# Layer 0, images 1 to 7: scores as three one-pass products of 12-bit halves, two units in a batch, one bank of sums

## The chip, the cores and the metric

The kernel runs on one core of a Trainium2 chip. The metric is the device time of one execution in microseconds. Engines are named as in the profile: PE (TensorE: matmuls; PEld its weight loads), DVE (VectorE), ACT (ScalarE), POOL (GpSimd) and SP, whose queue issues nearly all DMAs. All work in parallel and meet at semaphores.

## The reference

Two layers act on 8 images of 384 channels and 32 x 32 = 1024 positions. Only the attention of layer 0 is touched:

```python
qkv = (tokens @ qkv_w + qkv_b).reshape(b, n, 3, NUM_HEADS, HEAD_DIM)   # n 1024, 8 heads of 48
q, k, v = (qkv[0], qkv[1], qkv[2])
attn = jnp.einsum('bhnd,bhmd->bhnm', q * scale, k)
attn = attn + _relative_bias(h, w, mlp_w1, mlp_b1, mlp_w2, mlp_b2)[None]
attn = jax.nn.softmax(attn, axis=-1)
out = jnp.einsum('bhnm,bhmd->bhnd', attn, v)
```

`tokens` is the image after a group norm. An output projection with a residual follows, then layer 1 (attention and a binarized feed-forward net), which this change leaves alone.

## The kernel before

**Units.** Heads go in four pairs, one head on partitions 0 to 63 and one on 64 to 127. Pairs 0 to 2 hold six heads; pair 3 (`NF0`) holds the last two, whose channels are computed as 16 spare rows beside each of the other heads (rows 48 to 63 of a half) and moved into place by DMA (`FR` = 16 rows at a time). A unit is a pair, a half of the 512 queries (`h`) and 256 of the keys (`m2`), two key tiles of 128. An image has 4 x 2 x 4 = 32 units.

**Scores and sums.** `scores` (L748) lays four tiles of 48 x 64 into PE's array at a time: two heads on its row halves, two runs of 64 keys on its column halves, in float32. DVE adds the position bias (L759, 128 x 1024, one instruction a head), ACT takes the exponential (L763). `weigh` multiplies the exponentials with v (L779), again in four tiles of 64 x 64: the two halves of the keys are summed in two PSUM banks, of which ACT copies one (L787) and DVE adds the other (L790). Row 0 of each head's result is the softmax's denominator, since v has columns of ones. `weigh` runs `LAG` = 2 units behind `scores`, so that PE always has sums to do while scores pass through DVE and ACT. PSUM has four buffers of two banks for everything: one holds the sums, three go round.

**Division.** When a pair is done, `divide` stores the denominators (L805), reads them back over 128 partitions (L807), inverts them on POOL (L808), stores and spreads them (L812, L820) and multiplies (L824). For pair 3 six DMAs (L834) then move rows into the spare rows of the others, for the output projection. These steps are spaced by `later`, a list of work due after so many calls of `later.step()`, one call a unit or a projection step.

**The next image's projections.** `Ahead` splits the normalized image into a high part (a mask on the bits, `mask`), a low part and a mixed part, each kept in a format that PE multiplies in one pass (`F32R`), and multiplies it with weights split in the same manner (`products`, L170). `BLOCKS` lists six blocks: three pairs, each for q and k. A block's products of mixed parts are in `pm`, those of high and low parts in `pg`; `take` joins them: ACT writes -`pm`/4096 + bias (L671), DVE adds `pg` (L675), two DMAs of 64 KB move the spare rows to pair 3 (L680). After three blocks `project_v` computes v (L700; DVE L708, L712), then the other three blocks follow. The image's scores start right after. The tiles of q and k lie in the pool `a_qk`: four buffers of 2 x 1024 numbers a partition, one for each pair. They also hold the image's high parts before.

**Order.** Every engine runs its instructions in the order in which the program issues them; the pools' buffers and the semaphores come from the framework. A buffer is given to a new tile when all that use the old one are done. Beside the units run, at fixed numbers: the loading of the next image (L343, `i` = 1), its group norm, the output projection of the image before (L847, at `i` = 3, 15.6 us of PE), the cutting of layer 1's weights (images 1 to 3) and the masks and roundings of the next image (`i` = 25 to 30). Image 0 has its own simpler projection (`project_qk`).

Of the kernel before, what the change touches and what calls it, by code (L numbers as in the profile page):

```python
# [22 lines left out]
ALU = mybir.AluOpType  # L23
# [251 lines left out]
def _layer0(tc, ins, x1, sums, shared, weights, beside):  # L275
# [9 lines left out]
    with ExitStack() as ctx:  # L285
        const = ctx.enter_context(tc.tile_pool(name="a_const", bufs=1))
        qkp = ctx.enter_context(tc.tile_pool(name="a_qk", bufs=NP0))
# [273 lines left out]
        def project_qk(b, xn):  # L561

            qk = {
                pair: qkp.tile([P, 2, N], F32, tag="qk", name=f"qk{b}_{pair}") for pair in range(NP0)
            }
            for pair in range(NF0):
                t = qk[pair]
                for s in range(2):
                    pq = mm2(f"pq{b}_{pair}_{s}")
# [11 lines left out]
                    if s == 0:  # L581
                        nc.vector.tensor_scalar(
                            t[:, s], flat2(pq), bias, D0**-0.5, ALU.add, ALU.mult
                        )
                    else:
                        nc.scalar.activation(t[:, s], flat2(pq), AF.Identity, bias=bias)
                    later.step()
                for j in range(2):
                    nc.sync.dma_start(
                        qk[NF0][j * S0 + pair * FR : j * S0 + (pair + 1) * FR],  # L590
                        t[j * S0 + D0 : (j + 1) * S0],
                    )
# [31 lines left out]
        class Ahead:  # L624
# [4 lines left out]
            def __init__(self, b, xn):  # L629
                self.b, self.xn = b, xn  # L630
                self.qk = {}
                self.parts, self.ps = [[], [], []], {}

            def tile(self, pair):
                if pair not in self.qk:
                    self.qk[pair] = qkp.tile([P, 2, N], F32, tag="qk", name=f"qk{self.b}_{pair}")
                return self.qk[pair]

            def high(self, k):
                return self.tile(k // 2)[:, k % 2]  # L640

            def mask(self, k):
                _masked(nc, self.high(k), self.xn[:, k])

            def round(self, k):
                t = etile(f"xh{self.b}_{k}", dtype=F32R)
                nc.scalar.copy(t, self.high(k))
                self.parts[0].append(t)

            def low(self, k):  # L650
                t = etile(f"xl{self.b}_{k}", dtype=F32R)
                nc.vector.tensor_sub(t, self.xn[:, k], self.high(k))
                self.parts[1].append(t)

            def mixed(self, k):
                t = etile(f"xd{self.b}_{k}", dtype=F32R)
                _mixed(nc, t, self.parts[1][k].bitcast(F32), self.high(k))
# [8 lines left out]
            def take(self, n):  # L666
                pair, s = BLOCKS[n]
                t = self.tile(pair)[:, s]
# [9 lines left out]
                last = self.tile(NF0)  # L678
                for j in range(2):
                    nc.sync.dma_start(  # L680
                        last[j * S0 + pair * FR : j * S0 + (pair + 1) * FR, s],
                        t[j * S0 + D0 : (j + 1) * S0],
                    )
                later.step()
# [56 lines left out]
        def scores(b, qk, u, weigh):  # L741
            pair, h, m2 = u
            s = [mm2(f"s{b}_{pair}_{h}_{m2}_{j}") for j in range(2)]
            for i in range(2):
                for c in range(2):
                    for j in range(2):
                        rows = slice(j * S0, j * S0 + D0)
                        nc.tensor.matmul(  # L748
                            s[j][ts(c, QP), i], qk[pair][rows, 1, ts(4 * m2 + 2 * i + c, QP)],
                            qk[pair][rows, 0, ts(h, HALF)], start=True, stop=True,  # L750
# [18 lines left out]
        def weigh(b, u, es):  # L769
# [24 lines left out]
            return finish  # L794

# [131 lines left out]
        for k, at in enumerate(((17, 22, 23), (21, 25, 26), (27, 30, 31))):  # L927
            for when, stage in zip(at, cut_weights_v(k)):
                later.after(when + 1, stage)
        for b in range(B):  # L930
            held = []
            for i, u in enumerate(units):
                done = held.pop(0) if len(held) == LAG else None
                held.append(
                    (u, scores(b, qk, u, lambda: weigh(b, *done) if done else None))
                )
                if i == (16 if b == 0 else 1) and b + 1 < B:
                    xn = load(b + 1)
                    for at, stage in zip(
                        (2, 3, 4, 6, 9, 10, 11) if b == 0 else (5, 6, 7, 10, 13, 13, 13),  # L940
# [35 lines left out]
            def weigh_held():  # L976
                finish = weigh(b, *held.pop(0))
                if finish is not None:
                    finish()
# [14 lines left out]
            weigh_held()  # L994
# [25 lines left out]
            qk = ahead.qk  # L1020
# [1352 lines left out]
```

## Time and profile before

| | us |
|---|---|
| median of 3 runs | 2943.4 (2942.52 to 2945.47) |
| profiled execution, its time | 2940.6 |
| its span in the trace | 2939.1 |
| PE busy | 2913.6 |
| DVE, ACT, POOL busy | 1969.8, 1504.5, 493.5 |
| one image of layer 0 (period of the stages) | 166.0 |
| of it: 32 units, output projection, next image's projections | 112.8, 15.6, 37.5 |
| score products (L748), sums (L779), all 8 images | 606.4, 603.5 |

The span is the time from the first to the last instruction in the trace; the 1.5 us to the execution's own time lie around it. Busy times of PE are those of matmuls that are pipelined, so a busy PE may still not be at its peak. In all 1060 DMAs move 209 MB.

### The profile page before, as it was taken

The numbers are of one execution on the slowest core, as the hardware profiler recorded it, in microseconds if no ns is written. First come the engines' busy times: TensorE is split into PE (matmuls) and PEld (weight loads), VectorE is DVE, ScalarE is ACT, GpSimd is POOL, SyncE is SP. The second block draws the span as 40 slices with busy tenths as digits, with TensorE's granted clock in tenths as the row PEclk, the third lists the DMA queues.
The fourth block names the chain that finished last, engine by engine and source line by source line (L and its number), as shares of the span: only waits on it lengthen the run. The fifth ranks groups of instructions, "written<-read, shape, count | busy, mean of one in ns | idle before, by whom it ended". The sixth has DMA issues, their size and how long they took to land.

```text
span 2939.1 us, 47521 instructions
## 1 busy us (share of the span) xinstructions
PE 2913.6 (99%) x19538; PEld 1703.0 (58%) x19538; DVE 1969.8 (67%) x1999; ACT 1504.5 (51%) x1846; POOL 493.5 (17%) x318
## 2 busy tenths in 40 slices
PE   8999999999999999999999999999999999999998
PEld 3465665657575666634546647647647647655553
DVE  3976758586676757573655775875875875875756
ACT  2644636264444636363643655555555555564644
POOL 3121202021110202012202202302302302311020
PEclk9999999999999999999999999999999999999999
DMA  7642131413122130323311212112112112112111
GB/s 191 197 147 84 50 111 46 121 45 98 47 74 73 39 113 24 100 69 107 78 56 31 84 31 72 67 32 72 67 32 72 67 32 72 67 40 83 40 46 39
DMA packets 131970, 214.35 MB, mean 73 GB/s; under 512 B 62144, under 2 KB 81072, under 8 KB 130368
## 3 DMA queue, kind: packets, MB, share of 16 engines
q1 hardware_dynamic: 128480, 209.39, 24.3%
q8 instruction: 157, 2.57, 0.4%
q10 hardware_dynamic: 3264, 1.82, 0.2%
q14 instruction: 69, 0.57, 0.1%
HBM read 161.83 MB, written 40.28 MB: 69 GB/s over the span
## 4 chain that ended last, share of the span: by engine, by line
PE 92%; DVE 3%; DMA 2%; ACT 2%; issue 1%; SPq 0%; POOL 0%; DVEq 0%; ACTq 0%
PE s L748 15%; PE o L779 15%; PE s L1725 11%; PE o L1774 10%; PE pg L170 6%; PE y2p L2019 6%; PE y1p L1968 5%; PE pp L847 4%; PE pv L1662 4%; PE pm L170 3%; PE pp L1871 3%; PE vg L700 2%; PE pq L1514 2%; PE pq L572 1%; DMA rb<-rd 1%
## 5 line engine op out<-in xcount | busy, mean ns | idle before, releaser
L763 ACT ACTIVATE e<-e 128x1024 f32<-128x1024 f32 x512 | 534.5, 1057 | 333.2 <-DVE e L759 316.7
L759 DVE TENSOR_TENSOR e<-s,grow 128x1024 f32<-128x1024 f32 x512 | 601.1, 1218 | 154.6 <-PE s L748 137.8
L748 PE MATMUL s<-qk 48*64 48x512 f32 x4096 | 606.4, 590 | 1.8 <-DVE e L759 1.8
L779 PE MATMUL o<-e,v 64*64 64x512 f32 x4096 | 603.5, 589 | 0.0
L1736 ACT ACTIVATE e<-s,kc 128x512 f32<-128x512 f32 x768 | 463.3, 693 | 173.5 <-PE s L1725 163.9
L1725 PE MATMUL s<-qk,qk 64*64 64x512 f32 x3072 | 419.4, 592 | 1.6 <-DVE oT L1784 1.3
L1774 PE MATMUL o<-e,v 64*64 64x512 f32 x3072 | 415.0, 590 | 0.0
L748 PEld LDWEIGHTS s<-qk 48*64 48x64 f32 x4096 | 231.7, 132 | 235.3 <-issue 98.7
L779 PEld LDWEIGHTS o<-e,v 64*64 64x64 f32 x4096 | 251.6, 133 | 188.4 <-issue 97.3
L1725 PEld LDWEIGHTS s<-qk,qk 64*64 64x64 f32 x3072 | 154.3, 132 | 191.5 <-issue 109.0
L1751 DVE TENSOR_TENSOR t<-t,e 128x1024 f32<-128x1024 f32 x192 | 230.9, 1221 | 45.6 <-ACT e L1736 45.4
L1774 PEld LDWEIGHTS o<-e,v 64*64 64x64 f32 x3072 | 160.5, 133 | 168.2 <-issue 141.9
L808 POOL TENSOR_TENSOR inv<-sums,over 128x16 f32<-128x16 f32 x32 | 95.8, 2992 | 843.9 <-DMA sums<-sd 776.8
L1955 DVE TENSOR_REDUCE parts<-y 128x1 f32<-128x1024 f32 x75 | 89.7, 1217 | 102.6 <-ACT y L1952 102.1
L1748 DVE TENSOR_TENSOR t<-e,e 128x1024 f32<-128x1024 f32 x96 | 114.0, 1224 | 58.8 <-ACT e L1736 58.7
L1631 POOL TENSOR_TENSOR hc<-hc,rsqrt 128x32 f32<-128x32 f32 x24 | 136.7, 5696 | 2.0
L1662 PE MATMUL pv<-wv,bx 128*128 128x384 f32 x384 | 128.3, 491 | 0.0
L1871 PE MATMUL pp<-oT,L_attn_proj_wT 128*128 128x512 f32 x288 | 126.3, 595 | 1.9 <-DVE oT L1837 1.8
L847 PE MATMUL pp<-oT,wp 128*128 128x512 f32 x288 | 125.7, 595 | 0.0
L1662 PEld LDWEIGHTS pv<-wv,bx 128*128 128x128 f32 x384 | 119.4, 314 | 9.8 <-ACT e L1736 4.1
L675 DVE SCALAR_TENSOR_TENSOR qk<-pg,qk 128x1024 f32<-128x1024 f32 x42 | 51.4, 1225 | 100.3 <-PE pg L170 74.2
L1968 PE MATMUL y1p<-lun,w 128*128 128x512 f32 x360 | 113.5, 396 | 3.0 <-DVE lun L1918 3.0
(225 smaller groups left out, 3583.8 us busy)
## 6 DMA issues: line engine op xcount, KB each, us to landing
rb<-rd SPq DMA_DIRECT2D x110, 256.0 KB
wc<-there SPq DMA_DIRECT2D x25, 576.0 KB
wc<-cut SPq DMA_DIRECT2D x24, 576.0 KB
xn<-in_x_dram SPq DMA_DIRECT2D x24, 512.0 KB
res<-in_x_dram SPq DMA_DIRECT2D x24, 512.0 KB
x<-res SPq DMA_DIRECT2D x24, 512.0 KB
bx<-x SPq DMA_DIRECT2D x8, 1536.0 KB
rq<-hi SPq DMA_DIRECT2D x48, 256.0 KB
```

The source lines that it names most:

```text
L170: self.nc.tensor.matmul(out[:, h], w[:, i, k], part[k][:, ts(h, HALF)], start=(k == 0 and i != 1), stop=(k == KC - 1 and i != 0),)
L748: nc.tensor.matmul(s[j][ts(c, QP), i], qk[pair][rows, 1, ts(4 * m2 + 2 * i + c, QP)], qk[pair][rows, 0, ts(h, HALF)], start=True, stop=True,)
L759: nc.vector.tensor_add(e.rearrange("p (i q) -> p i q", i=2), s[j], bass.AP(near.tensor, near.offset, [near.ap[0], [-QROWS * IW, 2], [1, HA ...
L763: nc.scalar.activation(e, e, AF.Exp)
L779: nc.tensor.matmul(po[ts(j, S0), r], v[keys, 2 * m2 + i, 2 * pair + j, :], es[j][keys, ts(i, HALF)], start=(m2 == 0 and i == 0), stop=(m2 ...
L847: nc.tensor.matmul(pps[b, m][:, h], (wp[:, k] if k < NF0 else wl)[:, ts(m, P)], oT[:, k, ts(h, HALF)], start=(k == 0), stop=(k == (NF0 if ...
L1662: nc.tensor.matmul(pv[:, i, 0:C], xt[:, k].rearrange("c (p m) -> c m p", m=MT)[:, 2 * m2 + i], wv[:, k], start=(k == 0), stop=(k == KC - 1),)
L1725: nc.tensor.matmul(s[j][ts(c, QP), i], qk[pair, 1][rows, ts(4 * m2 + 2 * i + c, QP)], qk[pair, 0][rows, ts(h, HALF)], start=True, stop=True,)
L1736: nc.scalar.activation(e[:, ts(i, HALF)], s[j][:, i], AF.Exp, scale=kc[:, pair, j, m : m + 1])
L1751: nc.vector.tensor_add(total[j], total[j], e)
L1774: nc.tensor.matmul(po[ts(j, D1), r], v[keys, 2 * m2 + i, at : at + D1], es[j][keys, ts(i, HALF)], start=(m2 == 0 and i == 0), stop=(m2 == ...
L1968: nc.tensor.matmul(py[m][:, h], w1[:, k, ts(m, P)], un[k][i][:, ts(h, HALF)], start=(k == 0 and i == 0), stop=(k == KC - 1 and i == 1),)
```

## The change

It concerns images 1 to 7. Image 0 keeps `scores` and `weigh`; its q and k tiles only become single ones.

- **Halves.** `take` ends with two more instructions: ACT copies q or k into a one-pass tile (`high`), DVE subtracts it (`t` becomes the low half). Both halves go to a DRAM tensor `there`, with the rows of pair 3 put in place on the way: six DMAs a block, two of 512 KB and four of 64 KB, in place of the two from tile to tile.
- **Loads.** `load_k` reads a pair's k back as three tiles, `load_q` one half of its q as two. A tile has 64 rows a head, 48 for the head's channels and 16 that are free: the three products of (q0, k0), (q0, k1), (q1, k2) are filled so that together they give (high + low) x (high + low). `load_k` has 12 DMAs of 64 to 192 KB (1.5 MB), `load_q` 8 (512 KB).
- **Buffers.** `a_qk` has eight buffers of 1024 numbers a partition, the same memory. A pair needs three for k and one for each half of q; a block in `take` needs two until its stores are done.
- **Batches.** `Batches.run` does four key tiles of a pair and a query half, that is two units. One key tile takes 3 passes for each head, 64 rows x 128 columns of the array. Three PSUM buffers hold three key tiles; the fourth goes to the first one's banks (for the second batch of a half one head's scores go to the free bank beside the sums). DVE adds the bias, now to both heads of a key tile at once, except where the banks are apart (`split`, two instructions of 512); ACT takes the exponential.
- **Sums.** `weigh` multiplies all 128 keys at once, 128 x 64 tiles, so that both heads' sums are in one bank. ACT's copy is all; the addition of DVE is gone. In a batch the second half of the batch before is weighed, then the first half of this one.
- **Order.** `load_q` of a pair's second half and `load_k` of the next pair are issued at the end of its first batch, `load_q` of the next pair at the end of its third. The loads for an image's first pair come after `project_v` and ahead of the last three blocks. At an image's end one half batch of sums is left, where two units were. Some group norm steps move by a few units.

```diff
-        qkp = ctx.enter_context(tc.tile_pool(name="a_qk", bufs=NP0))
+        qkp = ctx.enter_context(tc.tile_pool(name="a_qk", bufs=2 * NP0))
...
             def take(self, n):
                 pair, s = BLOCKS[n]
-                t = self.tile(pair)[:, s]
+                name = f"{self.b}_{pair}_{s}"
+                t = qkp.tile([P, N], F32, tag="qk", name="t" + name)
+                high = qkp.tile([P, N], F32R, tag="qk", name="th" + name)
...
-                last = self.tile(NF0)
+                nc.scalar.copy(high, t)
+                nc.vector.tensor_sub(t, t, high.bitcast(F32))
+                for x, part in enumerate((high.bitcast(F32), t)):
+                    nc.sync.dma_start(self.there[s, pair, x], part)
+                    for j in range(2):
+                        nc.sync.dma_start(
+                            self.there[s, NF0, x, j * S0 + pair * FR : j * S0 + (pair + 1) * FR],
+                            part[j * S0 + D0 : (j + 1) * S0],
+                        )
+                later.step()
+
+            def load(self, to, s, pair, cols, pieces):
+
                 for j in range(2):
-                    nc.sync.dma_start(
-                        last[j * S0 + pair * FR : j * S0 + (pair + 1) * FR, s],
-                        t[j * S0 + D0 : (j + 1) * S0],
-                    )
-                later.step()
+                    for row, n, x, at in pieces:
+                        nc.sync.dma_start(
+                            to[j * S0 + row : j * S0 + row + n].bitcast(F32),
+                            self.there[s, pair, x, j * S0 + at : j * S0 + at + n, cols],
+                        )
+
+            def load_k(self, pair):
+                name = f"{self.b}_{pair}"
+                self.k[pair] = [
+                    qkp.tile([P, N], F32R, tag="qk", name=f"k{i}" + name) for i in range(3)
+                ]
+                for t, pieces in zip(self.k[pair], (
+                    ((0, D0, 0, 0), (D0, FR, 1, 0)), ((0, D0, 1, 0), (D0, FR, 0, 0)),
+                    ((0, 2 * FR, 0, FR), (2 * FR, 2 * FR, 1, FR)),
+                )):
+                    self.load(t, 1, pair, slice(0, N), pieces)
+
+            def load_q(self, pair, h):
+                t = qkp.tile([P, 2, HALF], F32R, tag="qk", name=f"q{self.b}_{pair}_{h}")
+                self.q[pair, h] = t[:, 0], t[:, 1]
+                for part, pieces in zip(self.q[pair, h], (
+                    ((0, D0, 0, 0), (D0, FR, 1, 0)),
+                    ((0, 2 * FR, 1, FR), (2 * FR, 2 * FR, 1, FR)),
+                )):
+                    self.load(part, 0, pair, ts(h, HALF), pieces)
...
+        class Batches:
+            def __init__(self, b, halves, pairs):
+                self.b, self.halves, self.pairs = b, halves, pairs
+                self.po = mm2(f"o{b}")
+                self.held = []
+
+            def weigh(self):
+                at, pair, h, kt, es = self.held.pop(0)
+                po = self.po[:, at % 2]
+                for i in range(2):
+                    for j in range(2):
+                        nc.tensor.matmul(
+                            po[ts(j, S0)], v[:, kt + i, 2 * pair + j, :], es[i][:, ts(j, HALF)],
+                            start=(kt + i == 0), stop=(kt + i == MT - 1),
+                        )
+                if kt + 2 < MT:
+                    return
+                nc.scalar.copy(oT[:, pair, ts(h, HALF)], po)
+                if h == NH - 1:
+                    divide(self.b, pair)
+
+            def run(self, n, between):
+
+                at, g = divmod(n, 2)
+                pair, h = self.pairs[at // NH], at % NH
+                name = f"{self.b}_{pair}_{h}_{g}"
+                whole = [mm2(f"s{name}_{i}") for i in range(3)]
+                first = [[t[:, 0], t[:, 1]] for t in whole]
+                if g == 0:
+                    banks = first + [first[0]]
+                else:
+                    banks = first + [[self.po[:, 1 - at % 2], first[0][0]]]
+                k, q = self.halves.k[pair], self.halves.q[pair, h]
+                es = []
+
+                def products(i):
+                    for m, (a, c) in enumerate(((0, 0), (0, 1), (1, 2))):
+                        for j in range(2):
+                            nc.tensor.matmul(
+                                banks[i][j], k[c][ts(j, S0), ts(4 * g + i, P)],
+                                q[a][ts(j, S0)], start=(m == 0), stop=(m == 2),
+                            )
...
+                for i in range(3):
+                    products(i)
+                take(0, g == 1)
+                products(3)
+                for i in range(1, 4):
+                    take(i, g == 1 and i == 3)
+                if self.held:
+                    self.weigh()
+                self.held = [(at, pair, h, 4 * g, es[:2]), (at, pair, h, 4 * g + 2, es[2:])]
+                self.weigh()
+                between()
...
-                        (2, 3, 4, 6, 9, 10, 11) if b == 0 else (5, 6, 7, 10, 13, 13, 13),
+                        (2, 3, 4, 6, 9, 10, 11) if b == 0 else (5, 7, 9, 12, 15, 15, 15),
...
+                batches = Batches(b, ahead, (0, 1, 2, NF0) if b % 2 else (2, 0, 1, NF0))
+                halves = ahead
+                for n in range(len(units) // 2):
+
+                    def between(n=n):
+                        at, pair = n % 4, batches.pairs[n // 4]
+                        behind = batches.pairs[n // 4 + 1] if pair < NF0 else None
+                        if at == 0:
+                            halves.load_q(pair, 1)
+                            if behind is not None:
+                                halves.load_k(behind)
+                        elif at == 2 and behind is not None:
+                            halves.load_q(behind, 0)
+                        for i in range(2 * n, 2 * n + 2):
+                            beside_unit(i)
+
+                    batches.run(n, between)
+                held, weigh_held = batches.held, batches.weigh
...
-            weigh_held()
+            if b == 0:
+                weigh_held()
             ahead.low(2)
             ahead.load_weights_v(wh)
             weigh_held()
...
-            qk = ahead.qk
+                    ahead.load_k(order[1] // 2)
+                    ahead.load_q(order[1] // 2, 0)
```

## Prediction

> **What bounds the kernel now.** I read the page first: busy times, then the shares of the chain that ended last.
>
> ```profile
> PE 2913.6 (99%) x19538; PEld 1703.0 (58%) x19538; DVE 1969.8 (67%) x1999; ACT 1504.5 (51%) x1846; POOL 493.5 (17%) x318
> ...
> PE 92%; DVE 3%; DMA 2%; ACT 2%; issue 1%; SPq 0%; POOL 0%; DVEq 0%; ACTq 0%
> ```
>
> TensorE never rests, so in layer 0 a matmul removed is time won and a new wait of PE is time lost, both in full. Next the table by stage, for one image (they repeat every 166.0 us), in two answers:
>
> ```profile
> 688.10:725.60 37.50, 37.50 (x184) 32.24 (x182) 18.76 (x25) 6.95 (x7) 5.30 (x2) 1.00 0.46 122
> ```
> ```profile
> 725.60:737.10 11.50, 11.50 (x98) 4.84 (x98) 9.82 (x9) 6.80 (x7) 0.00 (x0) 1.00 0.75 252
> 737.10:752.70 15.60, 15.60 (x40) 6.71 (x42) 3.20 (x3) 1.65 (x2) 0.00 (x0) 1.00 0.23 93
> 752.70:854.00 101.30, 101.30 (x931) 59.73 (x931) 81.20 (x77) 64.85 (x67) 20.59 (x13) 1.00 0.09 23
> ```
>
> The first number after a window is its length, the second PE's busy time: equal everywhere. The 32 units of an image take 11.5 + 101.3 = 112.8 us, 7.05 us for two units; the 15.6 between is the output projection, the 37.5 the next image's projections. Then the chain in order of time across that boundary, and DVE's timeline there:
>
> ```profile
> 713.04 1.39 PE pm L170 x6
> 714.42 2.80 PE pg L170 x12
> ...
> 722.82 2.80 PE pg L170 x12
> 725.62 5.85 PE s L748 x45
> ```
> ```profile
> 725.73 1.22 DVE L675 SCALAR_TENSOR_TENSOR qk<-pg,qk 128x1024 f32<-128x1024 f32 x1 [2.98 <-PE pg L170]
> 727.55 6.88 DVE L759 TENSOR_TENSOR e<-s,grow 128x1024 f32<-128x1024 f32 x6 [0.60 <-PE s L748]
> ```
>
> The reader is to see two things. Twelve one-pass products last 2.80 us, 0.2325 each. And today one DVE instruction stands between the last projection and the first score add, while PE goes on with scores at once. Last, what prices the new pieces: SP's timeline, an issue group of small loads, and the only column-tiled product.
>
> ```profile
> 704.19 1.12 SPq L820 DMA_DIRECT2D rb<-rd  x2
> 705.41 0.52 SPq L161 DMA_DIRECT2D wc<-cut  x1
> 706.34 1.17 SPq L680 DMA_DIRECT2D qk<-qk  x2
> 707.61 0.52 SPq L161 DMA_DIRECT2D wc<-cut  x1
> 711.57 4.16 SPq L834 DMA_DIRECT2D oT<-oT  x6
> ```
> ```profile
> L486 SPq DMA_DIRECT2D wide<-table x64: 302/419/692, 38.1 to 73.5; - x64
> ```
> ```profile
> 2914.05 1.94 PE L1850 MATMUL sum<-f,ones 128*64 128x512 f32 x8
> ```
>
> **What the Trainium skill says.** "FP8 and Floating Point Precision", TensorE Precision Notes: a true float32 product is four passes, a reduced one is a single read. The trace agrees: L847 needs 15.65 us for 36 instructions, two to a product, so 0.87 us against 0.2325. "TensorEngine Tiling (Array Packing)", Key Properties: changing the tiling mode drains TensorE. It agrees: between L1774, L1850 and L1871 the first two starts after a change come about 0.15 to 0.2 us late in sum. "TensorE: Matmul & The Clock Gate", Architectural detail (the array is 16× 32×32): ScalarE and VectorE are strict FIFO. "DMA: Bandwidth & Descriptors", Anatomy of one DMA: a DMA's semaphore wait happens on its issuing sequencer. SP shows it above: nothing is issued from 708.1 until L834's wait for POOL ends at 711.57.
>
> **PE work, per batch of two units.** Removed: 8 rounds of score products and 8 of sums, the 7.05 us. Added: 4 key tiles x 3 passes x 0.2325 = 2.79, if the two heads' row tiles run together, as L748's four tiles do (starts 7 ns apart). Sums: 4 key tiles x 2 instructions x 0.4285 = 3.43; L1850's pairs start 0.423 to 0.429 apart, so full rows on half the columns cost what the four quarters cost. The array's shape now changes twice: 0.3. Within the batch, the fourth tile's bank comes free with the first add: 0.05 + 0.91 (three passes to the end of the last) + 1.22 + 0.1 = 2.28 against PE's 2.14; the first two exps end at about 4.5 when PE gets to them at 4.9. So 0.13 idle. Sum 6.65, gain 0.40 x 16 batches x 7 images = **45 us**. Bounds: 60 (shape change free) to 20 (0.25 us more idle or change per batch). DVE has 5.1 us of adds in 6.65 (the two split adds, 0.69 a half, included), ACT 4.5: both keep up. L790's 0.69 us addition goes and frees nothing that PE waits for.
>
> **The projections.** Each of six takes (B1 to B6) gets an ACT copy (1.03, row L647) and a DVE subtraction (1.22, row L652). Both queues are in order, so takes become a ping-pong: 1.12 + 1.23 + 1.03 + 0.1 = 3.5 us each. From the first product (t = 0), B1 to B3 have their second parts at 7.2, 8.6 and 10.0, so the subtractions end at 12.0, 15.6 and 19.1. V's results wait behind them on DVE, and V's third group, which needs the first's banks, starts at 21.4 instead of 19.2: with two waits of 0.4 before it V ends at 27.6 instead of 25.3, **2.3 us** of PE. Before t = 0 the last sums now wait for an exp of their own batch: **0.7**.
>
> **First batch of an image.** PE ends B6 at t = 40.2. Addition 1.23, copy 1.03, subtraction 1.22 must pass before DVE's first add: 43.8. Then two adds and an exp (3.7 with latencies) and 1.75 of sums: 49.2, where PE's own work ends at 44.75. Held sums that cover this today (LAG 2) are gone. **4.5 us.**
>
> **Buffer and SP.** `qk` has 8 one-image buffers. At B6 four hold the first pair's k and q, two each B4 and B5; B6's first ACT waits until B4's stores have landed. In SP's order these stand behind 20 loads (12 + 8), which stand behind L834's six copies. L834 starts today 24 us after t = 0; with the stores of B1 to B3 before it (18 issues, nearly 9 us of SP) 26 to 28. Six copies at 0.63, 20 loads at 0.464 (L486's median 0.419 and 0.045 between two), three stores 1.4, landing 2.1 (as L680's): 42.6 to 45. Without that wait B6's ACT would start at 38.4, its DVE part at 40.3; now 43.7 to 46. **4.4 us** more, bounds 0 and 6.
>
> **Loads within an image.** At a pair's start `load_q(pair, 1)` follows `divide` of the pair before on SP. The ACT copy ends 7.55 after the batch's start, two issues and their landing (L807 follows L805 by 1.55), L807 0.34, eight loads 3.5, landing 2.1: 15.0. The third pass of that half needs it at 13.9. 1.1 us, and a little for `load_q` of the next pair, at about 27.8 where 27.6 is the need: 1.2 x 3 pairs. In the first pair the output projection covers it. **3.6 us** an image, bounds 0 and 8. Bytes: 7.7 MB of stores and 10 MB of loads an image; the three 512 KB loads of L343 land 1.3 us apart, 400 GB/s, so bytes alone don't bind. L680's two copies a take go from SP.
>
> **Sum.** 7 x (0.7 + 2.3 + 4.5 + 4.4 + 3.6) = 108 lost, 45 won: +63. The profiled execution is 2940.6 us (span 2939.1); the runs' median stands 2.8 above it. 2940.6 + 63 + 2.8 = **3006 us**.
>
> **Rivals.**
> (A) The forecast: PE's saving is smaller than the new serial pieces. For it: 99% PE leaves no slack, and takes and first adds share two FIFO engines. 2965 to 3055.
> (B) Faster. The covers are better than I count: B4's stores are issued early enough and SP's waits end in time. Then 7 x (0.7 + 1.0 + 1.5) = 22 lost against 45 to 60: 2905 to 2925. Decided by when B6's first ACT starts: from t = 38.4 on, each us costs 7. For it: DMA engines are 46% busy there; against it: SP's order and the count of buffers.
> (C) Much slower: row tiles of 64 x 128 in one-pass format don't load weights together. L170's load lasts 0.188, two in series make a pass 0.376: 12 x 0.144 x 112 = 193 more, about 3200. No row shows this shape in this format; the two-row products of L445 do load two row tiles 7 ns apart. Decided by the interval of the score products: 0.23 or 0.38.
> (D) It doesn't do what it says: the products still take several passes, or both sums are not in step. Same sign and size as C; together one chance in twenty.
> (E) Gains and losses cancel to within 0.2%, about 6 us, which is what this measurement can tell from no change.
>
> **How the numbers follow.** A 0.63, B 0.24, C and D 0.05, E 0.08. A's own range is 2965 to 3055. The range reaches down into B to 2913 and ends at 3062, leaving out C, D and the edges of A and B. Faster 0.24, within 0.2% 0.07, slower 0.69.
>
> **What would show it.** Right: score products 0.23 apart in pairs; a batch near 6.65 us in mid-pair; PE idle in each image's first batch of 8 to 10 us, ended by DVE's first add behind a subtraction; B6's ACT waiting for a DMA; the third V group late by some 2 us. Wrong: no idle of PE at the image's start (B), PE at 0.38 a pass (C), or idle of PE inside every batch, which would say that I misjudged DVE's and ACT's slack.

## The result and the profile after

The changed kernel takes 3320.16 us (median of 4 runs, 3313.3 to 3321.22) against 2942.96 (2941.68 to 2945.47): 377 us more, a ratio of 1.1276, 95% interval 1.1256 to 1.1295. The forecast was 3006, range 2913 to 3062. The sign was right; the loss is six times the one forecast, and more than half of it (210 us, by the experiments below) comes from a wait that stood in no term of the forecast. The page of the kernel after, first busy times, then the chain that ended last by engine:

```profile
PE 2993.9 (90%) x16850; PEld 1670.2 (50%) x16850; DVE 1981.5 (60%) x2097; ACT 1553.7 (47%) x1888; POOL 492.8 (15%) x318
...
PE 72%; DVE 10%; DMA 6%; issue 4%; ACT 4%; SPq 3%; POOL 0%; DVEq 0%; ACTq 0%; POOLq 0%
```

PE has 2688 instructions fewer and is busy 80 us longer. In a span of 3318.9 us it rests some 325 us, and its mean granted clock is 0.97 where it was 0.999. The stages of one image, from the table of windows (length, busy time and count of PE, PEld, DVE, ACT, POOL, then PE's clock, DMA share, GB/s):

```profile
632.87:678.87 46.00, 38.78 (x180) 32.28 (x180) 23.07 (x29) 11.12 (x11) 5.30 (x2) 0.98 0.70 215
678.87:702.70 23.83, 17.58 (x73) 8.73 (x73) 11.72 (x12) 10.62 (x10) 0.00 (x0) 0.68 0.89 272
702.70:718.36 15.66, 15.66 (x38) 6.77 (x38) 2.57 (x2) 0.00 (x0) 0.00 (x0) 1.00 0.62 247
718.36:851.32 132.96, 104.40 (x569) 46.87 (x569) 79.86 (x89) 65.36 (x66) 20.64 (x13) 0.96 0.31 77
```

The first two numbers were equal in every stage before. Now the projections last 46.0 instead of 37.5, the first two batches 23.8, and the other fourteen 133.0, that is 9.5 each where 6.65 was forecast. The output projection, 15.66, is as it was. Most of the loss is inside the batches, in every one of them. The timeline, two batches, and one more batch 18 us later (start, duration, what; in brackets the engine's idle time before it and who ended it):

```profile
721.80 1.94 PE L845 MATMUL o<-e,v 128*64 128x512 f32 x8
...
725.24 0.57 ACT L851 COPY oT<-o 128x512 f32<-128x512 f32 x1
725.86 1.94 PE L845 MATMUL o<-e,v 128*64 128x512 f32 x8 [2.12 <-ACT oT L851]
...
732.21 0.68 DVE L882 TENSOR_TENSOR e<-o,grow 128x512 f32<-128x512 f32 x1
...
732.94 3.65 PE L845 MATMUL o<-e,v 128*64 128x512 f32 x16 [1.90 <-DVE e L882]
...
751.01 5.35 PE L845 MATMUL o<-e,v 128*64 128x512 f32 x16 [1.90 <-DVE e L882]
```

In a half's first batch, PE finishes one bank of sums (721.80) and should go on in the other. It starts there at 725.86, right when ACT has copied the **finished** bank. In the second batch it should add to the bank in use, and starts at 732.94, when DVE has read the score tile that lies in the **spare** bank beside it. Each time it waits for a bank that its own instruction doesn't touch. Both banks are one tile, `po`, and the waits are those of a tile. The last line adds the second price: the same 16 sums last 5.35 instead of 3.65, because in the clock records a spell of 3.41 us at half clock lies inside them. The list of waits gives the two sizes for the whole run (us in total, times, longest):

```profile
PE o L845 <- DVE e L882: 106.9, 56, 2.0
PE o L845 <- ACT oT L851: 104.1, 49, 2.1
```

And the start of an image, the engines' timeline, to be read with the forecast's steps:

```profile
678.90 3.38 PE L872 MATMUL s<-q,k 64*128 64x512 f32 x12 [5.74 <-DMA q<-halves]
...
682.26 1.11 ACT L668 ACTIVATE t<-pm,bqk 128x1024 f32<-128x1024 f32 x1 [11.41 <-DMA halves<-th]
...
683.43 1.65 PE L872 MATMUL s<-q,k 64*128 64x512 f32 x6 [1.14 <-ACT t L668]
...
688.16 1.65 PE L872 MATMUL s<-q,k 64*128 64x512 f32 x6 [3.08 <-DVE e L886]
```

PE waits three times: for the first pair's loads, for the third score buffer, which B6 still holds (ACT's step for it waited 11.41 us for a store), and for DVE's first addition.

### The profile page after: what moved, and what is told of

Its sections match the earlier page's. It is cut to its first block, busy times and chain, and to the rows that moved or that the text cites. A ratio compares the mean times of both kernels' runs of the same rounds, so it can differ in the third digit from the quotient of the medians.

```text
span 3318.9 us, 43621 instructions
## 1 busy us (share of the span) xinstructions
PE 2993.9 (90%) x16850; PEld 1670.2 (50%) x16850; DVE 1981.5 (60%) x2097; ACT 1553.7 (47%) x1888; POOL 492.8 (15%) x318
## 4 chain that ended last, share of the span: by engine, by line
PE 72%; DVE 10%; DMA 6%; issue 4%; ACT 4%; SPq 3%; POOL 0%; DVEq 0%; ACTq 0%; POOLq 0%
PE o L845 11%; PE s L1862 10%; PE o L1911 10%; PE s L872 9%; PE y2p L2156 5%; DVE e L886 5%; PE y1p L2105 4%; PE pp L956 4%; PE pv L1799 4%; PE pg L170 3%; PE pp L2008 3%; PE s L777 1%; DVE e L882 1%; PE pm L170 1%; PE o L808 1%
## 5 line engine op out<-in xcount | busy, mean ns | idle before, releaser
L890 ACT ACTIVATE e<-e 128x1024 f32<-128x1024 f32 x448 | 473.8, 1058 | 627.4 <-DVE e L886 358.1
L845 PE MATMUL o<-e,v 128*64 128x512 f32 x1792 | 459.2, 649 | 211.0 <-DVE e L882 106.9
L886 DVE TENSOR_TENSOR e<-s,grow 128x1024 f32<-128x1024 f32 x336 | 389.9, 1216 | 168.9 <-PE s L872 168.9
L872 PE MATMUL s<-q,k 64*128 64x512 f32 x2520 | 405.6, 435 | 71.1 <-DMA q<-halves 35.8
L1911 PE MATMUL o<-e,v 64*64 64x512 f32 x3072 | 414.2, 590 | 0.0
L872 PEld LDWEIGHTS s<-q,k 64*128 64x128 f32 x2520 | 257.1, 201 | 260.0 <-issue 137.8
L845 PEld LDWEIGHTS o<-e,v 128*64 128x64 f32 x1792 | 123.3, 144 | 481.5 <-issue 176.4
L882 DVE TENSOR_TENSOR e<-s,grow 128x512 f32<-128x512 f32 x168 | 110.3, 685 | 230.9 <-PE s L872 230.9
L1911 PEld LDWEIGHTS o<-e,v 64*64 64x64 f32 x3072 | 159.0, 133 | 169.8 <-issue 142.7
L933 POOL TENSOR_TENSOR oT<-oT,rb 128x1024 f32<-128x1024 f32 x32 | 76.6, 2395 | 330.7 <-DMA rb<-rd 263.0
```

The source lines that it names most:

```text
L845: nc.tensor.matmul(po[ts(j, S0)], v[:, kt + i, 2 * pair + j, :], es[i][:, ts(j, HALF)], start=(kt + i == 0), stop=(kt + i == MT - 1),)
L872: nc.tensor.matmul(banks[i][j], k[c][ts(j, S0), ts(4 * g + i, P)], q[a][ts(j, S0)], start=(m == 0), stop=(m == 2),)
L886: nc.vector.tensor_add(e.rearrange("p (j q) -> p j q", j=2), whole[i % 3], near(2 * pair, kt, h, [GW * IW, 2]),)
L890: nc.scalar.activation(e, e, AF.Exp)
L1911: nc.tensor.matmul(po[ts(j, D1), r], v[keys, 2 * m2 + i, at : at + D1], es[j][keys, ts(i, HALF)], start=(m2 == 0 and i == 0), stop=(m2 == ...
```

## The experiments

For ten of the kernels the table gives the mean of images 1 to 7 (from first matmul of a stage to first matmul of the next, read from the trace), the time, and how long layer 0 ran at half clock. "Batches" is all 16, without the output projection.

| kernel | projections | batches | half clock | time | ratio, 95% interval |
|---|---|---|---|---|---|
| before | 38.0 | 112.2 | 0 | 2942.96 | 1 |
| after | 46.9 | 157.4 | 198 | 3320.16 | 1.1276 [1.1256, 1.1295] |
| a1 no spare bank | 47.2 | 142.2 | 205 | 3215.89 | 1.0927 [1.0895, 1.0959] |
| a2 copy late | 46.8 | 145.7 | 259 | 3235.61 | 1.0994 [1.0962, 1.1026] |
| a3 both | 46.7 | 127.8 | 133 | 3110.07 | 1.0567 [1.0537, 1.0598] |
| b2 whole loads | 44.5 | 117.5 | 75 | 3024.32 | 1.0276 [1.0246, 1.0306] |
| c5 fewest issues | 39.9 | 118.0 | 44 | 2993.94 | 1.0173 [1.0144, 1.0203] |
| c8 last block elsewhere | 40.0 | 113.1 | 10 | 2964.21 | 1.0066 [1.0044, 1.0089] |
| c9 subtraction on POOL | 39.9 | 110.6 | 0 | 2944.92 | 1.0007 [0.9997, 1.0017] |
| c10: a3, last block elsewhere | 46.5 | 122.4 | 85 | 3082.63 | 1.0471 [1.0441, 1.0502] |

My theory after the result had two parts: W, the waits for the other bank of `po`, some 210 us by the list above; and S, the rest, made by SP's queue and the buffers at an image's start. The rival to W was that the clock, or DVE's and ACT's pace, sets the batch, and the waits only show it.

**a1_no_spare_bank.** No score goes to the spare bank; the fourth key tile always takes the first one's.

```diff
-                if g == 0:
-                    banks = first + [first[0]]
-                else:
-                    banks = first + [[self.po[:, 1 - at % 2], first[0][0]]]
+                banks = first + [first[0]]
...
-                take(0, g == 1)
+                take(0, False)
...
-                    take(i, g == 1 and i == 3)
+                    take(i, False)
```

> One part undone: in the second batch of a half the fourth key tile goes to the first one's two banks, as in the first batch, so no score lies beside the sums. Theory W (the sums tile is guarded as a whole: PE's sums wait for DVE's read of the score beside them, 106.9 us in the profile after, and for ACT's copy of the other bank, 104.1 us): the DVE half goes, less 0.15 us a batch for the fourth tile's own bank: 3320 - 95 = 3225, and the idle before the sums is put down to the ACT copy alone. Rival L (a batch is simply as long as DVE's and ACT's chain; the wait only shows where it ends): under 30 us gained, 3290 or more, with the idle before the sums put down to an exp.

Measured 3215.89, 104 us less than after, with PE's instructions the same in number (16850): the wait for DVE's reading of the spare bank is gone from the list, the one for ACT's copy is still 104.0 us in it.

**a2_copy_late.** The copy of the finished bank is issued after the sums that follow in the other bank.

```diff
-                nc.scalar.copy(oT[:, pair, ts(h, HALF)], po)
-                if h == NH - 1:
-                    divide(self.b, pair)
+
+                def finish():
+                    nc.scalar.copy(oT[:, pair, ts(h, HALF)], po)
+                    if h == NH - 1:
+                        divide(self.b, pair)
+
+                return finish
...
-                if self.held:
-                    self.weigh()
+                finish = self.weigh() if self.held else None
                 self.held = [(at, pair, h, 4 * g, es[:2]), (at, pair, h, 4 * g + 2, es[2:])]
                 self.weigh()
+                if finish is not None:
+                    finish()
```

> One part moved: ACT's copy of a finished sum (and the division's DMAs) is issued after the batch's second group of sums, in place of between the two groups. Theory W: the wait for the copy in each first batch (about 2.1 us, 104 us in all) goes, that for DVE stays: 3320 - 100 = 3220. Rival L: under 30 us gained, 3290 or more.

Measured 3235.61, 85 us less; 15 less gain than expected. Layer 0 has more time at half clock than without this edit, 259 us for 198. At half speed these 61 us are an estimated loss of up to 30, which is where the missing gain can have gone.

**a3_both.** Both edits.

> Both edits. Theory W: both waits go, a batch falls from about 9.2 us in mid-image to 6.7 to 7.2, PE's clock comes back: 3320 - 200 to 240, that is 3080 to 3120. What is left above the kernel before is then the boundary of the images and SP. Rival L: 3260 or more.

Measured 3110.07: 210 less than after, more than the two single gains together (104 + 85). W holds, and the rival falls as to DVE and ACT: neither was made faster. The clock is part of the gain.

That 210 meets the list's 211 so closely is partly luck. In the fourteen later batches 197 of the 211 us of waits stood, and 188 us were gained. There PE's waits fell from 28.3 us an image to 5.2, which is 162 of the 188: the two waits went, and 36 us of waits for loads and for DVE's additions took their place. The rest is the clock, which stands at half for 55 us less in these batches, an estimate of some 27 us at half speed.

That the chip needs no such wait between two banks is seen in the lines of a3 under b2: DVE reads score tiles from 889.24 to 893.78 while PE writes others from 890.44 on. The wait is taken away here by moving the instructions that made it; `po` as two tiles of one bank each, which would keep the change's own arrangement, wasn't tried, since the eight banks are taken by four buffers of two.

**b2_whole_loads.** a3, and each k and q tile is loaded by one transfer of 128 rows: the same bytes, 7 issues a pair instead of 28. The placing of rows in the tiles is left out of the computation, and the last pair is read from pair 2's rows.

```diff
-                for j in range(2):
-                    for row, n, x, at in pieces:
-                        nc.sync.dma_start(
-                            to[j * S0 + row : j * S0 + row + n].bitcast(F32),
-                            self.there[s, pair, x, j * S0 + at : j * S0 + at + n, cols],
-                        )
+                nc.sync.dma_start(to.bitcast(F32), self.there[s, min(pair, NF0 - 1), pieces[0][2], :, cols])
```

> As with both edits, but each tile of k and q is loaded by one DMA of 128 rows from one half (pair 3 from pair 2's rows), in place of four: the same bytes, 7 issues of SP a pair in place of 28. The placing of rows is left out, so the values are not the reference's. Theory S (at the image's start PE waits for SP's in-order issues: 5.7 us for the q loads and some 5 us for B4's stores behind 20 loads; and within an image for q): 8 to 13 us an image less than with both edits alone, 55 to 90 us, about 3025. Rival D (the bytes are what takes the time): within 20 us of it.

Measured 3024.32: 86 us less, so 28 small loads for 7 whole ones cost that much, at unchanged bytes. Only 15 of it (7 x 2.2) is in the projections; 10.3 us an image are in the batches. The windows of the fourteen later batches, a3 and then b2:

```profile
849.80:953.60 103.80, 99.90 (x570) 46.19 (x569) 74.74 (x70) 65.95 (x66) 20.60 (x13) 1.00 0.33 83
```
```profile
803.70:901.90 98.20, 97.53 (x569) 44.93 (x568) 74.70 (x70) 65.97 (x66) 20.65 (x13) 1.00 0.29 88
```

In this image the difference is 5.6 us (8.1 in the mean). The DMA engines are a third busy in both (0.33 and 0.29), so the loads' bytes don't fill them. a3's timeline shows where 3.15 of it come from, and it isn't a load that PE waits for:

```profile
878.91 3.61 SPq L690 DMA_DIRECT2D k<-halves  x8
...
886.82 0.31 SPq L521 DMA_DIRECT2D gs<-there  x1
...
888.52 0.79 DVE L527 BATCH_NORM_AGGREGATE gmv<-gs 32x2 f32<-32x144 f32 x1 [4.72 <-DMA gs<-there]
889.24 4.54 DVE L887 TENSOR_TENSOR e<-s,grow 128x1024 f32<-128x1024 f32 x4
...
890.44 0.96 PE L873 MATMUL s<-q,k 64*128 64x512 f32 x6 [3.15 <-DVE e L887]
```

Eight and twelve loads (L690) were issued one by one from 873.3 to 882.5, the last eight in the first line; a small transfer of the **next image's group norm** (L517, then L521) had to stand behind them. DVE waits 4.72 us for it at L527, the batch's additions are queued behind L527 on DVE, and PE behind the additions. Over the run DVE's wait at L527 is 27.2 us in a3, 9.3 in b2 and 0.7 before. It is 2.0 in the kernel after and 11.3 in c9, so such a wait costs only where DVE has no time to spare. PE also waits for loads itself in a3's later fourteen batches, 15.9 us in 24 times (0.6 in b2).

**c1_early_loads.** a3, with the first pair's loads of an image ahead of V's projection.

```diff
-                    for m2 in range(MT // 2):
-                        ahead.project_v(m2)
                     ahead.load_k(order[1] // 2)
                     ahead.load_q(order[1] // 2, 0)
+                    for m2 in range(MT // 2):
+                        ahead.project_v(m2)
```

> As a3_both (no score tile in the spare bank, the copy of the finished sums issued after the second half of them), and besides the first pair's 20 loads of an image are issued ahead of V's projection instead of behind it, so that they no longer stand behind the six copies of the last pair (which wait for POOL's multiplication) and no longer ahead of B4's and B5's stores. Theory S (what is left at an image's start is SP's order and number of issues: B6's ACT step waits for B4's stores, which stand behind the loads, and the first scores wait for the loads): the projections go from 46.7 to about 42 us and the first two batches from 21.7 to about 17, so 7 x 9 = 60 us less than a3_both's 3110: about 3050. Rival V (the rest of the projections is V's third group and the takes on two score tiles, DVE and ACT, not SP): within 15 us of a3_both, 3095 to 3110.

Measured 3128.01 (1.0629 [1.0598, 1.066]), 18 more than a3 and outside both ranges. The projections fell to 44.0, the first two batches rose from 21.7 to 25.8. In image 5 B4's stores were issued at 819.6, 5 us after the first scores began: now L945's six copies stand behind the 20 loads, and the stores behind both. ACT's step of B6 waited 15.08 us. Reordering a full queue moves the wait.

**c4_rows_placed_by_stores**, on c1, was to keep all of the computation and still need few loads: rows are put in place by the stores, so that a tile is read by one transfer, or two.

```diff
+                if len(pieces) == 1:
+                    of = self.there[s, pair, :, pieces[0] : pieces[0] + S0, cols]
+                    nc.sync.dma_start(to.bitcast(F32), of)
+                    return
+                for j in range(2):
+                    near = self.there[s, pair, j, pieces[0] : pieces[0] + 1, cols]
+                    of = bass.AP(near.tensor, near.offset,
+                        [[(pieces[1] - pieces[0]) * N, 2], [N, 2 * FR], near.ap[-1]])
+                    nc.sync.dma_start(to[ts(j, S0)].bitcast(F32), of)
```

> c1_early_loads, and the rows are put together when the halves are stored and not when they are loaded: the place in memory holds high rows 0 to 47, low rows 0 to 47 and high rows 0 to 15 again for each j, so that a tile is loaded by one transfer (or two, where it takes rows from two places): 10 loads a pair for 28, and 8 to 12 stores a block for 6. The issues of an image go from 148 to about 96, the bytes stay. Theory S: the batches of the middle go to b2_whole_loads' 97.8 us a 14 batches from 106, that is 7 x 8 = 56 us less than c1, and the first two batches lose another 1 to 2 us each time: 2970 to 3000. Rival B (bytes and not issues held a3's queue): no change against c1.

Measured 4214.25 (1.432 [1.4278, 1.4362]), a miss of more than 1200 us. One idle stretch of PE, from the windows:

```profile
742.00:762.00 20.00, 0.00 (x0) 0.00 (x0) 0.00 (x0) 0.00 (x0) 0.00 (x0) 0.57 0.13 50
```

Nothing runs, and the DMA share is 0.13: 2 of 16 engines. In the DMA records from 722 to 762 us exactly two packets are in flight for 90% of the time; in b2, while it loads (777 to 787 us), 12 to 16 for 70% of it. The sources here have two as their outermost extent, the halves `j` or the two pieces. **c6_high_stores_on_act** is c4 with the high halves' stores issued by ACT, and says nothing on its own question for that reason:

> c4_rows_placed_by_stores with the stores of the high halves issued by ACT's own queue, right behind the copy that rounds them, so that SP issues only the low halves. Theory S: SP's part at an image's start falls by another half, B6's ACT step comes 2 us earlier: 5 to 20 us less than c4. Rival A (4 to 6 issues of some 0.4 us are 2 to 2.5 us of ACT per block, and ACT's step, copy and issues then fill more than the 4.2 us that TensorE takes for a block): equal or up to 30 us more than c4.

Measured 4224.83 (1.4356 [1.4314, 1.4398]).

**d1_source_in_two_groups** tries the cause on b2, which has nothing else of c4:

```diff
+                near = self.there[s, min(pair, NF0 - 1), pieces[0][2], 0:1, cols]
+                of = bass.AP(near.tensor, near.offset, [[(S0 - 1) * N, 2], [N, S0], near.ap[-1]])
-                nc.sync.dma_start(to.bitcast(F32), self.there[s, min(pair, NF0 - 1), pieces[0][2], :, cols])
+                nc.sync.dma_start(to.bitcast(F32), of)
```

> b2_whole_loads (one transfer of 128 rows a tile, the placing of rows left out of the computation), with the source of each load given as two groups of 64 rows that can't be joined, because the second begins one row early (one more thing that the data leaves out): bytes, packets' size, number of issues and everything else as in b2. It asks why c4, whose loads are of this form, took 4214 us. Theory G (the transfer is dealt out to the DMA engines by the outermost extent of the source, so two groups are moved by two engines, each with 64 rows): a load of 512 KB takes some 11 us for 128 KB at b2's rate of about 12 GB/s an engine, that is 20 us or more; the time goes to about 4000 us or more, and the DMA share in the idle stretches is 2/16 = 0.13. Rival R (c4 suffered from its many small stores or from the gaps in its layout): within 30 us of b2's 3024.

Measured 4147.29 (1.4087 [1.4046, 1.4128]) against b2's 3024, with the same bytes and the same issues:

```profile
721.40:744.80 23.40, 0.00 (x0) 0.00 (x0) 1.90 (x3) 0.00 (x0) 0.83 (x3) 0.59 0.14 47
```

PE rests for 23.4 us, again with two engines' share of the DMAs. The Trainium skill states the rule ("DMA: Bandwidth & Descriptors", Why a DMA increments its semaphore by 16 and not by 1): a DMA uses the largest number of engines, at most 16, that divides the slowest extent of both its sides. With an extent of two that is two, and two of 16 is what c4 and d1 show.

**c5_fewest_issues.** b2 with the loads ahead of V, and without the four stores a block of spare rows, so that the last pair's own data is left out too.

> b2_whole_loads with the first pair's loads ahead of V's projection and without the stores of the blocks' spare rows (the last pair's halves are then never written; the placing of rows and the last pair's own data are left out of the computation, TensorE's work is unchanged): 40 issues an image. It bounds what SP's queue can give. Theory S: projections 39 to 41 us, first two batches 15 to 16, middle 97.5: 7 x (97.5 + 15.6 + 15.5 + 40) against 7 x (97.8 + 15.6 + 19.5 + 44.5) is 62 us less than b2's 3024, so about 2960, still above the kernel before (2942) by V's third group, the last block's subtraction ahead of the first addition and the two or three microseconds of low clock after an idle stretch. Rival V: 3010 to 3024.

Measured 2993.94, 34 more than the theory's 2960 and 16 below the rival's range, so neither held whole. The projections fell as expected, to 39.9; the first two batches, expected at 15 to 16, stayed at 19.8. The start of an image in c5's timeline says why:

```profile
745.84 4.11 SPq L935 DMA_DIRECT2D oT<-oT  x6
...
750.22 0.35 SPq L678 DMA_DIRECT2D halves<-th  x1
...
754.36 1.11 ACT L668 ACTIVATE t<-pm,bq 128x1024 f32<-128x1024 f32 x1 [4.92 <-DMA halves<-th]
755.51 1.23 DVE L672 SCALAR_TENSOR_TENSOR t<-pg,t 128x1024 f32<-128x1024 f32 x1 [4.81 <-ACT t L668]
755.53 0.96 PE L863 MATMUL s<-q,k 64*128 64x512 f32 x6 [2.39 <-ACT t L668]
...
757.84 1.23 DVE L676 TENSOR_TENSOR t<-t,th 128x1024 f32<-128x1024 f32 x1 [1.11 <-ACT th L675]
758.98 4.61 DVE L877 TENSOR_TENSOR e<-s,grow 128x1024 f32<-128x1024 f32 x4
...
760.26 1.65 PE L863 MATMUL s<-q,k 64*128 64x512 f32 x6 [3.77 <-DVE e L877]
```

B4's store is issued at 750.22, behind the six copies of L935. B6's ACT step needs the tile that this store reads and starts after 4.92 us of waiting; DVE's two steps follow one another, the first addition is third in the row, and PE waits 2.39 and 3.77 us.

**c8_last_block_elsewhere.** c5, with B6's two tiles taken from the pool of the scores, where the halves of x come free.

```diff
+                if n == self.last:
+                    t = etile("t" + name)
+                    high = etile("th" + name, dtype=F32R)
+                else:
                     t = qkp.tile([P, N], F32, tag="qk", name="t" + name)
                     high = qkp.tile([P, N], F32R, tag="qk", name="th" + name)
```

> c5_fewest_issues (same parts left out of the computation: the placing of rows and the last pair's own data), and the two tiles of each image's last block B6 come from the pool of the scores, where the halves of x that the projections have read come free, instead of the eight tiles that blocks, keys and queries share. Theory T (what is left at an image's start is the tile: B6's ACT step waits for B4's store to land, 4.9 us in c5, and TensorE's third score tile and its first exps wait for B6): first two batches from 20.0 to 15 or 16, 7 x 4 to 5 = 28 to 35 us less than c5's 2994: 2960 to 2966. Rival L (the first scores come no sooner, because DVE's additions then wait for the loads or for PE at low clock): 2985 to 2994.

Measured 2964.21: 30 less, the first two batches 15.3 instead of 19.8.

**c9_and_subtraction_on_pool.** c8, and B6's subtraction on POOL.

```diff
-                nc.vector.tensor_sub(t, t, high.bitcast(F32))
+                (nc.vector if n != self.last else nc.gpsimd).tensor_sub(t, t, high.bitcast(F32))
```

> c8_last_block_elsewhere, and B6's subtraction (high half from the whole) is done by POOL instead of DVE, so that DVE's first addition of the first batch no longer stands behind ACT's copy and this subtraction. In c5 the addition started 3.5 us after B6's addition had started, 1.2 of it the addition itself, so 1.05 for ACT's copy and 1.23 for the subtraction come out of the chain: 7 x 2.3 = 16 us less than c8, about 2945 to 2950, if the chain through DVE is what TensorE waits for. Rival: TensorE waits for the loads of the first pair, and it equals c8 within 4 us.

Measured 2944.92: 19 less, and within 0.2% of the kernel before. PE hardly waits at an image's start any more (0.4 us in the first two batches), as the windows of projections, first two batches and the other fourteen show:

```profile
857.10:896.90 39.80, 38.59 (x184) 32.48 (x182) 24.29 (x30) 12.13 (x12) 5.29 (x2) 1.00 0.73 249
896.90:909.50 12.60, 12.18 (x74) 5.67 (x73) 10.36 (x9) 9.52 (x9) 2.39 (x1) 1.00 0.91 330
925.10:1023.80 98.70, 97.34 (x569) 44.77 (x568) 74.67 (x70) 65.96 (x66) 20.79 (x13) 1.00 0.28 87
```

**c10_a3_last_block_elsewhere** makes the same edit in a3, where nothing is left out of the computation:

> a3_both (nothing left out of the computation, all 148 issues an image, loads behind V's projection) with B6's two tiles from the pool of the scores. Theory T: B6's ACT step no longer waits for B4's stores (14.7 us in a3's image 5) and first two batches fall from 21.7 to 17 or 18: 25 to 30 us less than a3's 3110, 3080 to 3085. Theory S (SP is the queue that the first scores and the later loads wait for, so that a free tile changes nothing): 3105 to 3110.

Measured 3082.63: 27 less than a3. So the tile is a cost of its own, with many issues or few. The first two batches fall from 21.7 to 13.9; part of that comes back, as the output projection behind them now takes 17.3 instead of 15.6 and the later fourteen batches 108.5 instead of 106.1.

The ladder is then 3320 - 210 (waits for the other bank) - 86 (issues of loads) - 30 (loads earlier, no stores of spare rows) - 30 (B6's tiles) - 19 (B6's subtraction) = 2945. It is one order of removal; in another the shares would differ, since each piece hides some of the next. No kernel here beats the one before. The nearest, c9, leaves out the placing of rows and the last pair's data, which a real kernel would have to pay for.

## Why the prediction was right and wrong

**Where it failed: the sum per batch.** The step "PE work, per batch of two units" wrote 0.13 us of idle into a batch of 6.65 us and held that DVE and ACT keep up. Their pace was judged rightly: in b2's later fourteen batches of 98.2 us DVE is busy for 74.7 and ACT for 66.0. What it never asked is what else the sums wait **for**. Of every tile that an instruction writes, all other users are candidates for a wait. `po` has two more: ACT's copy and, new with this change, DVE's addition from the spare bank. Some 2 us a batch is 211 us by the list of waits, and 210 by a3. The forecast had named its own falsifier, "idle of PE inside every batch"; its reason there, DVE's and ACT's slack, was the wrong one.

**The gain was a quarter of its size.** With the waits removed (c9) the batches of an image take 110.6 us against 112.2 (1.70 less before rounding): 0.11 a batch, not 0.40, so 12 us in all instead of 45, and outside the bounds of 20 to 60. The upper bound was also summed wrongly: with the shape change free the gain would be 0.70 a batch, 78 us. The products are as forecast: passes start 0.23 apart with both heads together (so C and D fall), the sums 0.43 a pair. The median batch in mid-image, in b2 as in c9, lasts 6.83 us for the 6.65 of the sum. In it the pass after the first one of a row follows by 0.34 instead of 0.23, twice a batch, and the fourth tile starts 0.40 after the ninth pass where 0.23 is the pace, so 0.17 of idle for my 0.13. The pause after a row's first pass, 0.22 in all, stood in no term and is the larger part; single longer batches, up to 7.9 us in c9, add to it.

**The projections** were forecast at 2.3 us more, with 0.7 for the last sums ahead of them, and are 9.0 more. Of this the V group is right in kind: c9 keeps 1.9 of 2.3, after everything else is gone, and PE's wait for DVE at V's third group is 1.15 us each image. For the 0.7 PE's list of waits has nothing. What was missing is PE's wait for the first pair's loads at the end, 35.8 us in seven images, 5.1 each. I had placed the loads on SP, but only asked what they delay, not when they themselves are needed. My own times had the answer: SP at L834 from 26 to 28, six copies, twenty loads and their landing come to 41 to 43, and PE is done with B6 at 40.2. A smaller piece is a load of the projections' weights (`wc`, L161), which stands on the same queue: 9.0 us, 1.3 an image.

**Buffer and SP, first batch.** Both mechanisms show as forecast. B6's ACT waits for B4's stores; a free tile is worth 4.3 us an image in c8 and 3.9 in c10, for 4.4. The subtraction and copy ahead of DVE's first addition are worth 2.7 (c9), for 4.5.

**Loads within an image** were forecast at 3.6 us, as lateness of q. In the kernel after nothing of it shows: by the list of waits PE never waits for a load in the later fourteen batches, of 9.5 us each. It appears when the batches get shorter. In a3 it is 2.3 us an image (15.9 in seven), within the bounds of 0 to 8, and PE waits 2.9 more for DVE's additions. All in all 28 loads a pair for 7 cost 10.3 us an image in the batches between a3 and b2, 8.1 of it in the later fourteen. In the image shown, 3.15 of it go through an instruction that I had not followed: L527, which belongs to the next image, waits for a transfer behind the loads. SP was counted for the attention's own transfers, and not for what else it carries.

**The clock** was no term at all. Half clock took 198 us of layer 0 after the change and none before, or in c9. At most half of that is lost time, as in the sums above, which lost 1.70 in a spell of 3.41. It can't be separated from the waits that it goes with: no run kept the waits at full clock.

Of the rivals, C's 3200 lies nearest to the time measured, but only by luck: its mechanism, passes 0.38 apart, isn't there. B (faster) needed all covers to hold; c9 gives it nearly all of them and ends at no change, since the batches gain 12 us (7 x 1.7) and the projections, with V's third group, take 13 (7 x 1.9).

## What to carry to other kernels

When a second use is put into half of a tile, ask for every user of the other half whether it must now wait: here the wait was kept for the whole tile. When transfers are added to a queue, follow every instruction that waits for anything on that queue, also of another stage, and what stands behind it on its engine. And where the engine that bounds has no slack, price its gain from measured intervals between instructions, pauses and restarts included, before setting it against the losses.

## What the runs showed of the hardware

- A load of 256 or 512 KB whose source has two as its outermost extent is moved by 2 of 16 DMA engines: 4147 us for 3024 with the same bytes and issues (d1 against b2).
- PE's clock falls before it has idled for a whole window. "TensorE: Matmul & The Clock Gate", What's actually happening, has half clock after at least one idle window of about 3.4 us. The spells here are one or more times 3.41 us long, which agrees. But of the 35 in layer 0 of the kernel after only six follow 3.41 us in which PE did next to nothing (busy 1.4% or less). In the 3.41 us ahead of the other 29 it was busy for 18 to 44% of the time. Ahead of the spell inside the line at 751.01 it idled for 1.9 us and worked the rest.
- The issue of a load from DRAM occupies SP for about 0.46 us when nothing holds it: L690's twelve of 64 to 192 KB take 5.46 us in a3 and 5.53 in c1. Size matters little: the median issue alone is 0.42 us for these, and 0.43 and 0.38 for b2's of 256 and 512 KB. A copy from tile to tile takes longer, L935's six in c5 0.69 each. So 20 loads keep everything else on that queue waiting for 9 us.
